# An eight-layer attention and feed-forward model on one core: the second attention's last batch by single tiles, with the next layer's short chain between its units, and four edits elsewhere

## The chip, the cores and the metric

The kernel runs as one program on one core of one Trainium2 chip. The metric is the device time of an execution in microseconds (us), and shorter is better. A measurement of this kernel can tell a difference of about 0.2% from none.

A core has five engines that work side by side, each through its own queue of instructions, in order: TensorE (PE, matrix products, with its weight loads shown apart as PEld), VectorE (DVE), ScalarE (ACT), GpSimd (POOL) and SyncE (SP), which here only starts transfers (DMAs). Matrix products land in PSUM, eight banks of 128 x 512 floats; everything else on chip lies in SBUF.

## The reference

Four batches of 256 tokens with 256 features (x) and of 512 context rows with 128 features (ctx) go through eight layers, all in float32. Each adds to x what it computes of the normalized x:

```python
x = x + L0_xattn(layernorm(x), ctx)    # a0: 16 heads of 16, q and k normalized per head
x = x + L0_ffn(layernorm(x))           # f0: 1024 hidden, the 2 largest of every 4 kept
x = x + L1_xattn(layernorm(x), ctx)    # a1: 16 heads of 128, rms norm of q and k per head
x = x + L1_ffn(layernorm(x))           # f1: below
x = x + L2_xattn(layernorm(x), ctx)    # a2: 16 heads of 128, keys and values shared by two
x = x + L2_ffn(layernorm(x))           # f2: 64 experts, 6 per token, and a shared one
x = x + L3_xattn(layernorm(x), ctx)    # a3: as a2
x = x + L3_ffn(layernorm(x))           # f3: 32 experts, 8 per token
```

The layer f1, which most of the change is about, takes the last token of each batch through a short recurrent chain, the thought, and gives it back to all tokens of its batch:

```python
x_norm = layer_norm(x, in_gamma, in_beta)
thought = x_norm[:, -1, :] @ agg_w + agg_b
for _ in range(4):
    t = layer_norm(thought, pn_gamma, pn_beta)
    t = gelu(t @ d1_w + d1_b)                    # 256 -> 1024
    thought = thought + (t @ d2_w + d2_b)        # 1024 -> 256
broadcast = (thought @ bc_w + bc_b)[:, None, :]
gate = sigmoid(x @ gate_w + gate_b)
return layer_norm(x + gate * broadcast, out_gamma, out_beta)
```

## The kernel before

x lies in SBUF as eight tiles of 128 tokens, two to a batch. The layers are methods of a class `Model` and are written one after the other. What is written first has precedence, but the framework that builds the program fixes the order of each engine's queue itself: it puts an instruction in front of an earlier one that it takes to be not yet ready, if the instruction's buffers are free. Generators (`drain(steps, n)` runs n steps of one) mix work of different stages by hand. A buffer is a slot of a pool; a new tile in a slot waits until the old one has been read for the last time. Pools that open later lie where closed ones lay.

- **Reciprocal roots** (`rsqrt`, L174). A scaling on DVE, then a power of -0.5 on POOL. Every norm uses it: that of tokens, of 128x1 numbers, that of a0's heads of 128x16, that of a1's heads of 128x4.
- **a0** (L245). For batch 0, `made(0)` makes keys and queries, with seven head norms, and `maxima(0)` the scores' maxima. Then `weighted(b)`, some twenty steps of exponentials and value products, runs beside `made(b + 1)` and `maxima(b + 1)`. `beside` (L600) says how many steps of one go with how many of the other (L634, L635).
- **a1** (L766). A group is a batch and four heads. Its unit is one head and one tile of tokens: scores (L833), maximum and exponential (L836, L837), and three units later `finish`: the division, four transposes on PE, and, when two heads of both tiles are there, `pair`: value products (L856) and output products (L865). While a group's eight units run, `prepare` makes the next group's keys and queries a step per unit (`head_rms`, L780).
- **f1** (L1098). Its weights are in three slots of 8 KB per partition, which f0 used before. All eight tiles are normalized and transposed; the four last tokens are gathered by four transfers from the normalized tiles (`last`, L1126); then comes the thought. Between its parts the generator `weight_products` (L900) multiplies a2's weights with each other (wqk and wvo, 28 steps with ten loads of 512 KB through two slots). After the thought, for each batch, `same` spreads its thought over 128 columns, `bc` multiplies it, and for each tile follow gate, sigmoid and the final norm on DVE (L1181 to L1189).
- **a2 and a3** (`gqa`, L950). Each batch begins with a norm and transposes (`begin`, L967), and then come units as in a1, with the queries of two heads at a time (L993). `step` (L1048) runs a step of one of two lists of generators after each unit. a3's `begin` first collects f2's outputs by indirect transfers of POOL (`collect`, L1250), and `fill` is what is left of a3's weight products.
- **f2's weights** (`f2_weights`, L1297) are asked for at a2's beginning, three groups of four experts ahead. **f3's** first weights (`Router.weights`, L1505) have three loads of 1 MB, written after a3's first batch (L1527).

## Time and profile before

| what | us |
|---|---|
| median of three runs | 2515.64 (2515.38 to 2515.76) |
| the profiled execution | 2529.95 |
| its span, first to last instruction | 2528.1 |
| PE busy in it | 2351.8 (93%) |
| DVE, ACT, POOL busy | 1315.4, 909.4, 412.9 |
| DMA mean over the span | 53 GB/s |

The stages' places in the span, by their first and last products on PE: a0's scores from 57.6, f0 from 436.7, a1's scores from 559.6, f1 between a1's last output products (1042.7) and a2's first queries (1165.1), f2's blocks of experts from about 1630, a3's first queries at 1859.7, f3's hidden products from about 2277.

A line of the profile that names a group reads: source line, engine, operation, output and input tiles (with buffer numbers left out), shapes, count, then busy time with the mean of one, then idle time of that engine just before them and what ended it. A line of waits reads: who waited, for whom, us in total, times, the longest. The granted clock is the share of full speed that PE was given. Many of the lines are those of helpers: L172 is every matrix product, L212 every transpose, L165 and L167 the copies out of PSUM, L158 most loads, L180 the power.

### The profile page before, as it was taken

To read this page: it belongs to the slowest core of one execution; us is meant where nothing else is said; L and a number is where in the kernel's file an instruction comes from. 1 tells how busy PE (TensorE), PEld (TensorE's weight loads), DVE (VectorE), ACT (ScalarE), POOL (GpSimd) and SP (SyncE) were. 2 spreads that over 40 slices of the span, in tenths; PEclk is the share of its full clock that TensorE was granted. 3 is DMA by queue.
4 is the path that set the end of the run, shared out by engine and by line. 5 is a ranking of instruction groups with operands and counts; after the bars stand their busy time and mean duration, and the time that the engine had idled before them with its cause. 6 is when DMAs were issued, how large, how long until landed. Compare 5 with 4: busy or idle time off the path is not lost. (4 is left out here: it accounts for less than half of the span.)

```text
span 2528.1 us, 28069 instructions
## 1 busy us (share of the span) xinstructions
PE 2351.8 (93%) x9918; PEld 1474.4 (58%) x9918; DVE 1315.4 (52%) x3490; ACT 909.4 (36%) x1912; POOL 412.9 (16%) x429
## 2 busy tenths in 40 slices
PE   4999998989999999896999999898889999999999
PEld 3555555555555555564656565587756566655555
DVE  5554453877777677526565665311245666641111
ACT  2324323235555555213434343133344344432111
POOL 7303300012212222001020101200120210002222
PEclk7999999999999999888999999999989999999999
DMA  7500001110000000213000000299720000005121
GB/s 233 173 1 1 1 1 37 64 46 1 1 1 1 1 1 1 54 42 104 2 26 1 26 1 25 74 251 267 241 87 2 26 16 11 1 10 162 50 62 35
DMA packets 102424, 134.94 MB, mean 53 GB/s; under 512 B 8272, under 2 KB 82760, under 8 KB 101768
## 3 DMA queue, kind: packets, MB, share of 16 engines
q1 hardware_dynamic: 97672, 120.51, 16.2%
q0 software_dynamic: 4608, 12.59, 1.6%
q8 instruction: 81, 1.33, 0.2%
q14 instruction: 63, 0.52, 0.1%
HBM read 96.50 MB, written 36.57 MB: 53 GB/s over the span
## 5 line engine op out<-in xcount | busy, mean ns | idle before, releaser
L172 PE MATMUL pv_a<-PT_a,ctx 128*128 128x512 f32 x768 | 352.4, 602 | 13.4 <-ACT PT_a L165 4.2
L1011 DVE CUSTOM_DVE_ANT_0 pr_a<-sc_a,mask_a 128x512 f32<-128x512 f32 x256 | 176.0, 688 | 229.3 <-PE sc_a L172 213.4
L172 PE MATMUL sc_a<-ctxT,qT_a 128*128 128x512 f32 x512 | 261.8, 596 | 5.1 <-issue 2.7
L172 PEld LDWEIGHTS pv_a<-PT_a,ctx 128*128 128x128 f32 x768 | 140.4, 191 | 183.7 <-issue 144.7
L1014 ACT ACTIVATE pr_a<-pr_a,sm_a 128x512 f32<-128x512 f32 x256 | 185.0, 723 | 122.6 <-DVE sm_a L1011 96.1
L1019 DVE TENSOR_SCALAR pr_a<-pr_a,sm_a,valid_a 128x512 f32<-128x512 f32 x256 | 140.1, 549 | 6.0 <-DVE sm_a L1018 0.2
L180 POOL TENSOR_TENSOR rstd_f<-rs_f,half 128x1 f32<-128x1 f32 (+1 forms) x36 | 19.2, 548 | 756.5 <-DVE rs_f L179 548.4
L172 PE MATMUL st<-a0qz,a0kT 128*128 128x256 f32 x512 | 132.4, 401 | 9.2 <-ACT pT L582 7.4
L1444 DVE TENSOR_TENSOR h<-u,gs 128x512 f32<-128x512 f32 x48 | 33.2, 691 | 202.3 <-POOL gs L1442 202.3
L172 PE MATMUL sc_a<-kT,qT 128*128 128x512 f32 x256 | 131.4, 595 | 1.3 <-ACT qT L801 0.8
L172 PE MATMUL sc_a<-a0kT,a0qz 128*128 128x496 f32 x256 | 121.1, 597 | 0.0
L172 PEld LDWEIGHTS st<-a0qz,a0kT 128*128 128x128 f32 x512 | 94.9, 197 | 42.6 <-ACT pT L582 22.5
L837 ACT ACTIVATE pr_a<-sc_a,sm_a 128x512 f32<-128x512 f32 x128 | 88.1, 688 | 85.4 <-DVE sm_a L836 84.1
L524 DVE TENSOR_REDUCE a0pad<-sc_a 128x1 f32<-128x496 f32 x128 | 85.8, 672 | 60.4 <-PE sc_a L172 60.0
L180 POOL TENSOR_TENSOR rr_a1k<-rs_a1k,half 128x4 f32<-128x4 f32 x64 | 64.6, 1009 | 320.0 <-DVE rs_a1k L179 290.1
L212 PEld LDWEIGHTS tp_a1p<-ident,pr_a 128*128 128x128 f32 x512 | 63.7, 141 | 67.2 <-issue 42.1
L212 PEld LDWEIGHTS tp_a3p<-ident,pr_a 128*128 128x128 f32 x512 | 64.0, 141 | 65.1 <-issue 50.7
L1441 ACT ACTIVATE gs<-g 128x512 f32<-128x512 f32 x48 | 28.7, 597 | 202.8 <-PE g L172 202.7
L167 DVE COPY xTb_f<-tp_xb_f 128x256 f32<-128x256 f32 x79 | 33.5, 424 | 129.8 <-PE tp_xb_f L212 129.8
L1000 ACT COPY qT_a<-q_a 128x512 f32<-128x512 f32 x64 | 37.5, 585 | 176.4 <-PE q_a L172 158.0
L212 PEld LDWEIGHTS tp_a2p<-ident,pr_a 128*128 128x128 f32 x512 | 63.9, 141 | 61.8 <-issue 48.8
L836 DVE TENSOR_REDUCE sm_a<-sc_a 128x1 f32<-128x512 f32 x128 | 87.4, 683 | 23.0 <-PE sc_a L172 22.9
(481 smaller groups left out, 4648.9 us busy)
## 6 DMA issues: line engine op xcount, KB each, us to landing
sent<-zero SPq DMA_DIRECT2D x6, 2048.0 KB
f2w<-in_L_w1T_dram SPq DMA_DIRECT2D x16, 704.0 KB
f2w<-in_L_w2T_dram SPq DMA_DIRECT2D x16, 704.0 KB
xb_f<-sent SPq DMA_DIRECT2D x20, 512.0 KB
back<-yb_f SPq DMA_DIRECT2D x20, 512.0 KB
cb_f<-f3comb SPq DMA_DIRECT2D x32, 192.0 KB
cb_f<-f3comb SPq DMA_DIRECT2D x32, 128.0 KB
f3wg<-in_L_wgT_dram SPq DMA_DIRECT2D x3, 1024.0 KB
```

What stands on the lines that cost most here:

```text
L167: self.nc.vector.tensor_copy(out, in_)
L172: self.nc.tensor.matmul(out, lhsT, rhs, start=n == 0, stop=n == last)
L180: self.last_pow = self.nc.gpsimd.tensor_tensor(out, t[:p, :n], self.half[:p, :n], ALU.pow).ins
L212: self.nc.tensor.transpose(ps[:, n * w : (n + 1) * w], block, self.ident[:w, :w])
L524: nc.vector.tensor_reduce(pad[:, h, HD : HD + 1], ps[:, :MAIN], AX.X, ALU.max, negate=True)
L836: nc.vector.tensor_reduce(st[:, 0:1], ps, AX.X, ALU.max, negate=True)
L837: nc.scalar.activation(pr, ps, AF.Exp, bias=st[:, 0:1], accum_out=st[:, 1:2])
L1000: nc.scalar.copy(qT, ps.rearrange("p (m t) -> p m t", m=2))
L1011: self.last_unit = nc.vector.tensor_tensor_reduce(pr, ps, mask, -1.0, -3 * NEG, ALU.add, ALU.min, accum_out=st[:, 0:1]).ins
L1014: nc.scalar.activation(pr, pr, AF.Exp, bias=st[:, 0:1], scale=-1.0, accum_out=st[:, 1:2])
L1019: nc.vector.tensor_scalar(pr, pr, st[:, 0:1], valid, ALU.mult, ALU.mult)
L1444: nc.vector.tensor_tensor(h, pu, t, ALU.mult)
```

## The change

Five edits are joined.

1. In a0's `made(0)`, `rsqrt` computes Sqrt on ACT and a reciprocal on DVE in place of the scaling and the power. A dictionary `roots` holds the two small constants and is emptied after `made(0)`.
2. `beside` in a0 runs one step of `weighted` with each step of `made` and with each five of `maxima`, instead of two with three and two with five.
3. The last batch of a1 runs in two passes over all sixteen heads, the second tile of tokens (the last tokens) first. `prepare` makes each group's keys in the first pass, keeps them for the second (two more buffers, `kept`) and makes the queries of one tile; two of its steps go with each unit. `four` replaces `pair` there: it works when four heads of one tile are there. When the last tokens' tile has its sum, f1's thought starts: `thinking` is a generator of 17 steps, and one runs after each unit that follows. f1's weights are asked for at a1's beginning (`load_f1`).
4. f1 normalizes the tiles, then mixes what is left of the thought with a2's weight products, three steps to one, computes the gates of all tiles, and only then `bc`. `out_beta` is added to x on POOL ahead, and the final norm is written as two fused DVE operations. The gate's multiplication is on POOL for the last three batches. Only batch 0's last steps are done in f1; the other six tiles' (`unfinished`) go between a2's first units, and f2's first three weight groups after them. Gates and normalized tiles lie where these groups will lie (`slots`).
5. f3's first loads are ordered behind the last load of a weight product (`last_product`), and in `gqa` the rest of a3's weight products (`fill`) is written ahead of the first batch's `begin`.

```diff
     def load(self, t, src):
-        self.nc.sync.dma_start(t, src)
+    def load(self, t, src, behind=None):
+        inst = self.nc.sync.dma_start(t, src).ins
+        if behind is not None:
+            self.tc.add_manual_dep(inst, behind, ORDER, reason="the other is wanted first")
+        self.last_load = inst.name
         return t
...
         p = var.shape[0]
+        if self.roots:
+            root = self.stats.tile([P, H], F32, tag="root", name=f"root_{name}")
+            self.nc.scalar.activation(root[:p, :n], var, AF.Sqrt, bias=self.roots[eps][:p], scale=scale)
+            self.nc.vector.reciprocal(out, root[:p, :n])
+            return
         t = self.stats.tile([P, H], F32, tag="rs", name=f"rs_{name}")
...
             drain(made(0))
+            self.roots = {}
...
-                    beside(steps, 2, made(b + 1), 3)
-                    beside(steps, 2, maxima(b + 1, "lane1"), 5)
+                    beside(steps, 1, made(b + 1), 1)
+                    beside(steps, 1, maxima(b + 1, "lane1"), 5)
...
+            def four(b, h, i, wT):
+                po = self.held(f"pv_a1_{b}_{h}_{i}")
+                self.matmuls(po, [(self.ctx[:, b, kt, :], wT[:, kt].rearrange("p h t -> p (h t)")) for kt in range(NKT)])
+                outT = p.tile([P, 2, S], F32, tag="outT", name=f"outT_a1_{b}_{h}_{i}").rearrange("p m (a t) -> p (m a) t", a=2)
+                self.copy(outT, po.rearrange("p (h t) -> p h t", h=4))
+                yield
+                if h == 3:
+                    self.total = self.longest(f"o_a1_{b}_{i}")
+                for m in range(4):
+                    nc.tensor.matmul(
+                        self.total[:, :D], outT[:, m, :], wvo[:, h - 3 + m, :],
+                        start=h == 3 and m == 0, stop=h == H - 1 and m == 3,
+                    )
+                if h == H - 1:
+                    self.add_to_x(b * NI + i, self.total[:, :D])
+                    if i == NI - 1:
+                        self.thoughts = self.thinking()
...
-            groups = [(b, hg) for b in range(B) for hg in range(H // HG)]
+            last_passes = ((NI - 1,), *((i,) for i in range(NI - 1)))
+            groups = [
+                (b, hg, which)
+                for b in range(B)
+                for which in ((tuple(range(NI)),) if b < B - 1 else last_passes)
+                for hg in range(H // HG)
+            ]
...
-                        drain(steps, 1)
+                        drain(steps, 1 if len(which) == NI else 2)
+                        if self.thoughts is not None:
+                            drain(self.thoughts, 1)
...
-            drain(begin(0))
             if fill is not None:
                 drain(fill)
+            drain(begin(0))
...
+    def thinking(self):
+        nc, p = self.nc, self.thought_pool
+        STEPS, NH, EPS = 4, 1024 // P, 1e-6
+        w, d1, d2, rows, d1b = self.f1_weights
+        last = p.tile([B, D], F32, name="last")
+        for b in range(B):
+            nc.sync.dma_start(last[b : b + 1, :], self.x[(b + 1) * (S // P) - 1][P - 1 : P, :])
...
+        yield
+        t = p.tile([B, D], F32, tag="t", name="t_in")
+        self.normalize(last, last, 1e-5, "f1last")
+        layer_norm(t, last, rows["in_gamma"], rows["in_beta"], "f1in")
+        yield
+        tT = columns(t, "f1in")
+        yield
+        thought = p.tile([B, D], F32, name="thought")
+        ps = self.work("agg")
+        self.matmuls(ps[:B, :D], [(tT[:, k, :], w[:, 0, k, :]) for k in range(NK)])
+        nc.vector.tensor_tensor(thought, ps[:B, :D], rows["agg_b"], ALU.add)
+        for step in range(STEPS):
+            t = p.tile([B, D], F32, tag="t", name=f"t_{step}")
+            layer_norm(t, thought, rows["pn_gamma"], rows["pn_beta"], f"f1_{step}")
+            yield
+            tT = columns(t, f"f1_{step}")
+            yield
+            ps = self.work(f"d1_{step}")
...
+            nc.scalar.activation(act, hid, AF.Gelu)
+            yield
+            ps = self.work(f"d2_{step}")
+            self.matmuls(ps[:B, :D], [(act[:, n, :], d2[:, n, :]) for n in range(NH)])
+            nc.vector.tensor_tensor(thought, thought, ps[:B, :D], ALU.add)
+            nc.vector.tensor_tensor(thought, thought, rows["d2_b"], ALU.add)
+        yield
+        self.thought_columns = columns(thought, "f1th")
...
+            while next(thoughts, "end") != "end":
+                drain(products, 3)
+            drain(products)
+            for i in range(NT):
+                ps = self.work(f"gate_{i}")
+                self.matmuls(ps[:, :D], [(self.tokens(xnT, k, i * P, P), w[:, 2, k, :]) for k in range(NK)])
+                nc.vector.tensor_tensor(gates[i], ps[:, :D], rows["gate_b"], ALU.add)
+                nc.scalar.activation(gates[i], gates[i], AF.Sigmoid)
+                nc.gpsimd.tensor_tensor(self.x[i], self.x[i], rows["out_beta"], ALU.add)
...
+            def last_steps(tiles):
+                for i in tiles:
+                    o = gates[i]
+                    nc.vector.tensor_tensor(o, o, xn[i], ALU.add)
...
+                    nc.vector.bn_stats(bn, o)
+                    nc.vector.bn_aggr(mv, bn)
+                    self.rsqrt(r, mv[:, 1:2], 1.0, EPS, f"f1o_{i}")
+                    nc.vector.scalar_tensor_tensor(o, o, mv[:, 0:1], out_gamma, ALU.subtract, ALU.mult)
+                    nc.vector.scalar_tensor_tensor(self.x[i], o, r, self.x[i], ALU.mult, ALU.add)
+                    yield
...
+                for i in range(b * NI, (b + 1) * NI):
+                    (nc.gpsimd if b else nc.vector).tensor_tensor(gates[i], gates[i], spread, ALU.mult)
+                if b == 0:
+                    drain(last_steps(range(NI)))
+            self.unfinished = last_steps(range(NI, NT))
...
+        load = lambda t, src: model.load(t, src, model.last_product if g == 0 else None)
```

## The prediction

> **What bounds the kernel now.** I read the page's slices first (is there an engine that is always busy, and where is it not), then busy time by stage, then what ended the waits in the stages where TensorE (PE) is not busy, then the DMA issues there.
>
> ```profile
> span 2528.1 us, 28069 instructions
> ...
> PE   4999998989999999896999999898889999999999
> ```
>
> PE is the bound nearly everywhere. A change gains only in the stretches below nine tenths: the first slice, slices 17 to 19 (the second feed-forward, f1) and some near slice 29. Busy time by stage, the columns being stretch, length, then PE, weight load, DVE, ACT, POOL, granted clock, DMA share, GB/s:
>
> ```profile
> 1042.70:1165.10 122.40, 86.24 (x412) 58.38 (x412) 58.57 (x195) 20.01 (x40) 11.03 (x21) 0.76 0.20 53
> ...
> 1062.00:1133.00 71.00, 65.56 (x332) 44.15 (x333) 20.66 (x56) 14.27 (x27) 2.12 (x4) 0.82 0.20 54
> 1133.00:1165.10 32.10, 10.90 (x42) 7.70 (x40) 27.87 (x107) 3.08 (x7) 6.26 (x12) 0.69 0.06 15
> 551.00:1042.70 491.70, 483.51 (x1912) 278.65 (x1911) 342.94 (x782) 253.53 (x526) 100.59 (x104) 1.00 0.00 1
> 57.50:434.00 376.50, 353.52 (x1683) 213.49 (x1682) 175.53 (x325) 131.43 (x243) 77.86 (x59) 0.98 0.11 35
> 0.00:57.50 57.50, 24.10 (x82) 17.78 (x83) 28.80 (x94) 14.59 (x28) 44.29 (x64) 0.75 0.73 222
> 1815.40:1859.70 44.30, 26.74 (x131) 18.40 (x129) 7.77 (x20) 15.48 (x28) 21.43 (x23) 0.81 0.73 238
> ```
>
> The second attention (551 to 1042.7) leaves PE 8 us. f1 (1042.7, the last output products of that attention, to 1165.1, the third attention's first queries) takes 122.4 us with PE busy 86.2 at a clock of 0.76: the middle is dense, the last 32 us belong to DVE. The start and the opening of the fourth attention (1815.4 to 1859.7) are half empty. What PE waits for in f1, and DVE in the start:
>
> ```profile
> PE tp_a L981 <- DVE xn_a L205: 11.1, 2, 10.1
> PE bc L172 <- DVE rs_f1o L179: 9.5, 1, 9.5
> PE tp_a2wk L212 <- DMA a2wk<-in_L_xattn_Wk_dram: 3.7, 1, 3.7
> ```
>
> ```profile
> DVE a0pad L380 <- POOL var_a0k L180: 9.4, 4, 3.1
> DVE a0pad L380 <- POOL var_a0q L180: 5.1, 2, 2.6
> DVE t_kd L372 <- PE ps_kd L172: 3.5, 1, 3.5
> DVE a0pad L380 <- POOL var_kd L180: 2.7, 1, 2.7
> ```
>
> In f1 it is DVE's eight last steps; in the start it is POOL's seven powers of 2.9 us. The SyncE queue in the fourth attention's opening has two of f3's three loads of 1 MB between the loads that PE waits for:
>
> ```profile
> 1819.86 0.46 SPq L158 DMA_DIRECT2D f3wg<-in_L_wgT_dram  x1
> 1823.32 0.37 SPq L158 DMA_DIRECT2D a3wq<-in_L_xattn_Wq_dram  x1
> 1826.54 0.35 SPq L158 DMA_DIRECT2D a3wv<-in_L_xattn_Wv_dram  x1
> 1826.94 0.43 SPq L158 DMA_DIRECT2D f3wu<-in_L_wuT_dram  x1
> 1839.46 4.36 SPq L158 DMA_DIRECT2D a3wo<-in_L_xattn_Wo_dram  x2
> ```
>
> The sum goes against the profiled execution, 2529.95 us (span 2528.1); the median of the three runs, 2515.64, is 14.3 lower, and I carry the difference over to it unchanged.
>
> **1. Start: Sqrt on ACT and a reciprocal on DVE for POOL's power.** Gone: seven powers of 128x16 (mean 2.90, 20.3 us of POOL) and seven scalings of 0.16 on DVE. Added: seven ACT operations like the 128x32 activation of f1 (0.23) and seven reciprocals like 128x16 at L509 (0.25); two memsets (0.1 each, nothing waits). DVE waited 17.2 us for the powers; a handover now costs about 0.6 (0.23, 0.25 and the starts), 4.2 in all: 13 us gained. ps_kd waited 3.5 for a POOL copy queued behind a power: 2 more. I take -15. At most both waits go, -20.7; at least half remains as waits for PE at its 0.75 clock or ACT's turn, -8. Sqrt needs a table load that the start does not have (1.283 us each); one falls before the first exponential, which at 56.27 is not what the first scores wait for.
>
> **2. First attention, one step of weighting for each other step instead of two for three (and for five).** The same work; about four more of the 20 steps of a batch lie under the making of keys and queries. In 57.5 to 434 PE is idle 23 us, of it 9.2 on th_a0k for a0pad and 7.4 on st for pT. If all of that went, -16; if the 32 maxima of 0.67 us, which get those steps no longer, wait instead, +7. I take -3, nearer to nothing, since 7.4 of it waits for ACT and stays.
>
> **3. Last batch of the second attention by tiles.** Scores, transposes, value products (four 512-wide per four units either way) and output products are the same in number. The first pass has all 16 key tiles and 4 query tiles beside 16 units instead of 32. By intervals of the timeline a unit holds PE 2.7 us (0.86 scores, 0.53 transposes, 0.86 values, 0.43 output), a key tile 1.4, a query tile 2.25: 74 us; DVE's share is 16 x 1.75 + 20 x 1.52 = 58, so PE stays the bound. Cost 0; up to +8 if the banks run short, -3 if the tail shrinks.
>
> **4. The thoughts inside it.** The generator begins at the fifth unit of the second pass, so 12 of its 17 steps run there: agg (1.9), three d1 (3.85 each), two d2 (3.6), four transposes (0.3) are 22 us on a PE with 8 us to spare: **+22**. Their DVE work (four norms of 2.3, adds) and three Gelus lie beside: ACT is busy 253 of 492. Each Gelu takes 0.23 and two loads of 1.283; exponentials behind it come 2.8 late, while a unit's result is used three units later. Stalls +3 (0 to +15; the upper end is four norm chains of 4.3, the time from L1167 at 1099.05 to tp_f at 1103.35, less their overlap). The row after a load shows no more than the load: 1171.32 plus 1.28, next activation 1172.62. The Trainium skill (ScalarE: Activation LUTs, What ACT_TABLE_LOAD costs) puts a switch at about 2.66 us, with a drain of 1.38, and its rule, to batch by table set, speaks against a Gelu between exponentials. By that figure the six switches would hold ACT 16 us instead of 7.7; the sum is the same as long as PE does not wait.
>
> **5. f1.** PE work left at full clock: 16 transposes 2.1, 32 gate products 6.8, weight products 22.3 (48 transposes at 1.04 for eight, 64 at 2.05 for sixteen, 16 at 1.98 for four), the last five thought steps 12, bc 3.4: 46.6 us. At a clock of 0.85 (0.82 now in the dense part) 55. Add the old 2 us of output products, 2 for the first load, and the end: bc to queries. That is spread 0.4, two tiles' multiply, add, statistics 2.3, aggregate and scale 0.3, power 0.7, two fused steps 0.8, then statistics to xn 1.7, transposes and copy 1.3, with 1 for POOL: 8.6. Together 68 us against 122.4: **-54**, at best -66 (clock 0.95, end under the products), at least -38. Two covers: the first load of a2wk goes out behind four loads of 0.43 instead of eleven and the four rows of `last` (issue 1052.57), so its 3.7 us mostly go; if not, +3.7 is in the bound. And POOL gets eight adds and six multiplies of 128x256 (0.72 each, row L457): behind them queue the two powers of the third attention's first norm, at worst 4.3 us late, 1 taken. The Trainium skill (SBUF — State Buffer, Summary: rules for kernel authors) says that DVE with two SBUF inputs and a GpSimd operation that reads SBUF block each other, the later fully. By that, 10 us of POOL work could hold DVE as long; no row here shows such a block.
>
> **6. Third attention.** Six last steps (two adds or statistics of 0.41, 0.3 of small ones, two fused of 0.48: 2.1 us) fall into the first seven units: 12.6 us of DVE, where DVE is busy 26.7 of 50 and 27 us hold 12.4 free. +3 (0 to 12.6). f2's first weight groups are asked for some 30 us later; they are wanted at 1630.
>
> **7. Fourth attention's opening.** f3's 3 MB go behind the last a3wo, the products ahead of the first norm. f3 begins about 2277, so its loads have 400 us of cover; without it, 10 us at 300 GB/s. PE needs 22.3 for the products from 1815.5; with 1 us between groups and first waits of 3, the queries could begin at 1848.7 instead of 1859.7. The gathers (12 of 1.3 on POOL from 1820.4, then norm, transposes, copy) allow 1842.1 at best. -11 (-17.6 to +3, if the norm's transposes now wait behind wvo).
>
> **Sum:** -15 - 3 + 22 + 3 - 54 + 3 - 11 = -55: 2475 profiled, **2460** as median.
>
> **Rivals.** (a) Load-bound products: each 512 KB took 3.7 (a2wo, 1115 to 1119) to 6.8 us (a2wq, 1053.2 to 1060) from issue to use, two at a time; ten at 6.8 are 34 us where PE needs 22: +12, 2472. For it: PE waited for a2wo; against: gates and thoughts can fill. (b) Start and fourth opening don't move, because the load of the weights and the gathers end last there: +26, 2486. Against: POOL's powers are what DVE waited for. (c) More: start -20, f1 at its best: 2443. (d) Slower: in the last batch the four work banks run short, since a norm holds one from matmul to multiply (0.86, 0.69, 0.68, 0.15, 1.0, 0.69 and handovers, 4.5 us) and 1.25 of them come per unit, beside a score bank for 2.5: 8.1 bank-us per unit, 2.0 over four banks, against 4.6 of PE. It decides once each of the 32 units loses 1.75 us; at 2.5 each, 80 us, the median is 2541. (e) The reordering is undone by the queues' fixed order, no change: 2516.
>
> **How the numbers follow.** Likeliest 0.42 (2460, alone 2449 to 2470), a 0.20, b 0.14, c 0.15, d 0.06, e 0.03. The range goes from below c to above b, 2432 to 2490; only d, e and tails lie outside. Faster by over 0.2%, which is what runs of this kernel can tell from none: 0.91; same 0.03; slower 0.06.
>
> **What would show it.** First scores near 42 instead of 57.6; the second attention 20 to 30 us longer with Gelus before its end; f1, from output products to queries, 60 to 75 us with no gap like 9.5 at bc; f3wg issued after the last a3wo and first queries there about 33 us after the first a3wk transposes. Wrong it is if the second attention grows by over 45, if the powers' waits return as waits for ACT, or if f1 shows DMA waits at every product.

## The result and the profile after

| | before, us | after, us | ratio, 95% interval |
|---|---|---|---|
| first set of runs (medians of 4 each) | 2515.51 (2514.96 to 2515.76) | 2471.55 (2465.20 to 2476.43) | 0.9826 (0.9803 to 0.9849) |
| third set of experiments, another chip (medians of 9 and 5) | 2537.19 (2525.57 to 2540.55) | 2490.99 (2477.24 to 2493.99) | 0.9823 (0.9799 to 0.9847) |

The change makes the kernel 44 to 46 us faster. The forecast was 55 (2460); its range held the time. As the stages show, the nearness is in part luck: errors of opposite signs met in the sum.

The page of the changed kernel, its first lines:

```profile
span 2463.4 us, 28085 instructions
...
PE   7999998989999999988999999898899999999999
```

PE's first slice has gone from four tenths to seven and f1's deepest slice from six to eight. Busy time by stage, the columns being stretch, length, PE, weight load, DVE, ACT, POOL, granted clock, DMA share, GB/s:

```profile
1047.90:1122.70 74.80, 54.65 (x256) 40.43 (x255) 32.59 (x98) 17.92 (x34) 16.25 (x25) 0.79 0.48 130
522.70:1047.90 525.20, 510.39 (x2045) 293.79 (x2046) 348.90 (x810) 257.05 (x529) 99.96 (x106) 0.99 0.00 1
39.60:397.80 358.20, 345.97 (x1683) 211.44 (x1682) 174.12 (x325) 133.78 (x246) 76.26 (x58) 0.99 0.12 43
0.00:39.60 39.60, 21.35 (x83) 16.18 (x84) 30.25 (x95) 16.10 (x36) 23.79 (x55) 0.87 0.83 262
1756.60:1796.00 39.40, 26.74 (x129) 18.54 (x128) 9.91 (x26) 15.48 (x28) 21.60 (x22) 0.83 0.68 211
```

These are f1, the second attention, the first attention, the start, and the fourth attention's opening. f1 still leaves PE 20.2 us idle, the opening 12.7. Cut at the first and last products of each stage on PE (and, for the opening, at the second half of the a3wk transposes), the two profiles compare so:

| stage | forecast of the difference | before | after | difference |
|---|---|---|---|---|
| start, to the first scores | -15 | 57.6 | 39.6 | -18.0 |
| first attention, to its last output products | -3 | 376.9 | 358.2 | -18.7 |
| f0 and the second attention's opening | 0 | 125.1 | 124.9 | -0.2 |
| second attention, first scores to last output products | +25 | 485.1 | 525.2 | +40.1 |
| f1, to the third attention's first queries | -54 | 120.4 | 74.9 | -45.6 |
| third attention, to its last output products | +3 | 429.3 | 412.7 | -16.6 |
| f2, to the second half of a3wk | 0 | 221.1 | 221.2 | +0.1 |
| fourth attention's opening, to its first queries | -11 | 44.2 | 39.4 | -4.8 |
| fourth attention and f3 | 0 | 668.5 | 667.4 | -1.1 |

They add up to the 64.7 us between the two spans, which is some 20 more than the medians say. The third attention's 16.6 was not expected and has to be explained first.

What DVE waits for in the start now:

```profile
DVE bn_a L216 <- DMA x<-in_x_dram: 2.1, 1, 2.1
DVE a0bvs L646 <- PE columns L371: 1.4, 1, 1.4
DVE t_kd L390 <- PE ps_kd L182: 1.1, 1, 1.1
DVE var_a0k L395 <- ACT sq_a0k L392: 1.0, 2, 0.5
```

POOL's powers are gone from that list, and the wait for ACT that takes their place is 1.0 us. What PE waits for in f1 now:

```profile
PE tp_a L1046 <- DVE mv_a L217: 6.1, 1, 6.1
PE tp_a2wk L227 <- DMA a2wk<-in_L_xattn_Wk_dram: 4.0, 1, 4.0
PE a2wvo L182 <- DMA a2wo<-in_L_xattn_Wo_dram: 3.5, 3, 1.9
PE tp_f L227 <- DVE mv_f L217: 2.5, 2, 2.3
```

The 9.5 at bc is gone, and of the 11.1 at the third attention's norm 7.2 are left (6.1 here, and 1.1 further down the list); the rest are loads and f1's own norms. SyncE's queue in the fourth attention's opening:

```profile
1765.31 0.37 SPq L165 DMA_DIRECT2D a3wq<-in_L_xattn_Wq_dram  x1
...
1772.15 0.38 SPq L165 DMA_DIRECT2D a3wo<-in_L_xattn_Wo_dram  x1
...
1778.86 10.30 SPq L165 DMA_DIRECT2D a3wo<-in_L_xattn_Wo_dram  x3
1789.21 0.50 SPq L165 DMA_DIRECT2D f3wg<-in_L_wgT_dram  x1
```

f3's loads are behind the last a3wo, as forecast.

### The profile page after: what moved, and what is told of

Same layout as the page of the kernel before. It is cut to its first block, busy times and chain, and to the rows that moved or that the text cites. A ratio compares the mean times of both kernels' runs of the same rounds, so it can differ in the third digit from the quotient of the medians.

```text
span 2463.4 us, 28085 instructions
## 1 busy us (share of the span) xinstructions
PE 2340.3 (95%) x9918; PEld 1472.9 (60%) x9918; DVE 1309.6 (53%) x3474; ACT 919.7 (37%) x1926; POOL 404.0 (16%) x435
## 5 line engine op out<-in xcount | busy, mean ns | idle before, releaser
L182 PE MATMUL st<-a0qz,a0kT 128*128 128x256 f32 x512 | 126.6, 392 | 6.7 <-ACT pT L600 4.3
L195 POOL TENSOR_TENSOR rr_a1k<-rs_a1k,half 128x4 f32<-128x4 f32 x64 | 64.7, 1012 | 309.4 <-DVE rs_a1k L194 284.0
```

The lines of the kernel that those rows point to most:

```text
L182: self.nc.tensor.matmul(out, lhsT, rhs, start=n == 0, stop=n == last)
L195: self.last_pow = self.nc.gpsimd.tensor_tensor(out, t[:p, :n], self.half[:p, :n], ALU.pow).ins
```

## The experiments

My theory after seeing both traces: the gain is the start and the first attention (36.7), and the last batch with its thoughts gives back most of what f1 wins. Rivals: the third attention really is faster; the first attention is shorter only because of the start before it; the second attention's growth is the thoughts alone.

The stages of every profile, in us (the kernels are told below; "opening" is the fourth attention's; the fourth attention itself was 410.2 to 411.4 and f3 257.0 or 257.1 in all of them):

| kernel | start | 1st att. | f0 | 2nd att. | f1 | 3rd att. | f2 | opening |
|---|---|---|---|---|---|---|---|---|
| e_before_again | 57.6 | 375.6 | 125.0 | 485.1 | 121.1 | 411.3 | 222.2 | 44.2 |
| e_beside_alone | 57.9 | 359.1 | 125.0 | 484.5 | 120.5 | 411.8 | 227.5 | 46.2 |
| e_no_roots | 58.0 | 360.8 | 126.3 | 525.2 | 71.5 | 412.5 | 225.9 | 41.5 |
| e_without_a1f1 | 40.5 | 359.9 | 126.4 | 484.5 | 120.7 | 411.2 | 221.6 | 39.5 |
| e_thoughts_late | 39.6 | 359.5 | 126.2 | 498.5 | 130.6 | 411.4 | 226.3 | 40.6 |
| e_gates_first | 39.5 | 359.7 | 126.2 | 525.1 | 67.1 | 410.9 | 222.5 | 40.3 |
| e_beta_later | 37.9 | 353.6 | 124.9 | 526.8 | 70.6 | 412.7 | 227.2 | 40.3 |
| e_both_f1 | 38.8 | 360.0 | 126.2 | 528.4 | 66.1 | 411.1 | 228.2 | 42.6 |
| e_f3_loads_free | 42.5 | 356.5 | 124.9 | 526.8 | 70.3 | 431.6 | 229.4 | 44.4 |
| e_begin_first | 42.4 | 356.7 | 124.9 | 525.1 | 74.9 | 429.9 | 223.4 | 41.4 |
| e_after_again | 39.7 | 358.1 | 124.9 | 525.1 | 71.5 | 431.1 | 217.9 | 39.3 |
| e_best | 41.6 | 358.9 | 126.4 | 525.7 | 66.7 | 427.1 | 227.8 | 40.8 |

The first four ran on one chip, the next four on a second, the last four on a third.

**e_before_again: the kernel before, profiled again.** No edit.

> The kernel before, profiled once more. In the profile of before, three stretches of the third attention (1300 to 1350, 1400 to 1450, 1500 to 1550), where POOL sends f2's rows, have PE idle for 4.0 to 5.0 us each, 13.9 us in the stage; the profiled execution stands 14.3 us above the median. Theory: these stalls belong to that one execution and not to the kernel. Then this profile, if it is near the median of 2515.5, has the third attention (first queries to last output products) at about 415 instead of 428.9. Rival: they belong to the kernel before, and the change took them away. Then they are here again, the stage is 428.9, and the profiled execution is again some 14 us above the median or the median holds them too. The time itself: 2515 to 2516 by both.

Measured: 2515.47 (2507.03 to 2523.22, ten runs) against 2519.18 (2511.05 to 2528.48) for the same kernel beside it, ratio 0.9989 (0.9965 to 1.0013). Two of the three stretches in which POOL sends f2's rows, first in the profile that the prediction was made from, then here (columns as above):

```profile
1300.00:1350.00 50.00, 45.98 (x181) 28.32 (x180) 27.47 (x106) 17.91 (x40) 11.96 (x12) 0.97 0.09 32
1400.00:1450.00 50.00, 45.01 (x180) 27.59 (x179) 29.51 (x119) 17.81 (x42) 11.78 (x12) 0.97 0.09 32
```

and the same two in this experiment:

```profile
1300.00:1350.00 50.00, 50.00 (x202) 30.85 (x201) 32.15 (x119) 21.20 (x47) 11.96 (x12) 1.00 0.09 32
1400.00:1450.00 50.00, 49.98 (x203) 30.93 (x202) 31.56 (x119) 21.20 (x47) 11.77 (x12) 1.00 0.09 32
```

The same kernel does the same work with the stalls and without. In the last set all four profiles, of four different kernels, have the third attention at 427 to 432; in the two sets before it all eight have it at 411 to 413. The times of the kernel before go the same way: 2519 and 2513 in the first two sets, 2537 in the last. So it goes by the set, that is by the chip or the hour, and not by the kernel: the third attention is the same in both, and the profile that I predicted from had 17 to 18 us in it that the changed kernel's profile had not. The record does not say on which chip that profile was taken. Without the stage's 16.6 the spans differ by 48, near what the medians say. What differs there stays open. The experiment also says how well a time can be told: ten runs of the kernel against fifteen of itself have an interval of 0.48%, more than the 0.2% that the prediction started from; and f2's stage, which was to stay as it is, went from 217.9 to 229.4 between the profiles.

**e_beside_alone: the kernel before with edit 2 alone.**

```diff
-                    beside(steps, 2, made(b + 1), 3)
-                    beside(steps, 2, maxima(b + 1, "lane1"), 5)
+                    beside(steps, 1, made(b + 1), 1)
+                    beside(steps, 1, maxima(b + 1, "lane1"), 5)
```

> The kernel before with only the two numbers of beside changed (one step of weighting with each step of making, instead of two with three; one with each five maxima instead of two). My prediction gave this edit -3: 2513. The traces say that the first attention's body (first scores to last output products) fell from 376.5 to 357.8. Theory: the edit alone does that, by 18.7: 2497, with the waits of th_a0k for a0pad down from 9.2 to about 2 and those of st for pT from 7.4 to about 4. Rival: the body is shorter since the start before it is (the clock and the first loads), then it stays above 370 here and the time is 2510 to 2515.

Measured: 2499.51, ratio 0.9911 (0.9883 to 0.9939); the first attention takes 359.1 instead of 375.6 on the same chip, with the start at 57.9. The rival is out. The first attention as a stretch in this run:

```profile
57.90:417.00 359.10, 347.26 (x1683) 211.97 (x1682) 173.82 (x324) 132.32 (x243) 76.39 (x59) 0.98 0.11 36
```

and two of its waits:

```profile
PE st L172 <- ACT pT L582: 3.9, 3, 1.6
PE th_a0k L391 <- DVE a0pad L380: 2.0, 1, 2.0
```

In the first profile of before the two waits were 7.4 and 9.2, and PE was busy 353.9 us for the same 1683 products (57.6 to 434.5). So of the 17.8 between the two stages 11.1 are idle time and 6.7 are PE's busy time. Against e_before_again, on the same chip, it is 16.5, of which 11.3 are idle (23.1 to 11.8) and 5.2 busy (352.5 to 347.3). The products themselves did not get shorter: one of st takes 396 ns in both, one of sc 601 and 602. So their records overlap more when there are fewer waits between them; why the busy time falls by just this much is not shown.

**e_no_roots: the changed kernel with POOL's powers back.**

```diff
-            for eps in (EPS, 1e-5):
-                self.roots[eps] = one([P, 1], f"eps{eps}")
-                nc.vector.memset(self.roots[eps], eps)
```

> The changed kernel with POOL's powers back in the making of batch 0. Theory (and my prediction's first step, 15): first scores at 57.6 again instead of 39.6, 15 to 18 us more than the changed kernel, 2487 to 2490. Rival: the start of the span is bound by loads or the clock, and most of the shift comes back in the body of the first attention: under 8 us more, below 2480.

Measured: 2489.25, ratio 0.9877 (0.9835 to 0.9919), 29.9 under the kernel before on that chip, where the whole change was 44 and 46 under it on others: by this edit 1 is worth 14 to 16, but that compares chips, and the interval here is 10 us to either side. The profiles say it more surely: the first scores are at 58.0 here, as in the kernel before (57.6 to 57.9), and at 37.9 to 42.5 wherever the edit is in, at 40.5 on this chip; the stages behind show nothing that comes back. The rival is out.

**e_without_a1f1: the kernel before with edits 1, 2 and 5 alone.** The diff is that of these edits above.

> The kernel before with edits 1, 2 and 5 alone (start, beside, the fourth attention's opening); the second attention's last batch, the thoughts and f1 are as before. By the stages of the two profiles these three edits are worth 18.0, 18.7 and 4.8, the rest of the change 5.5: 2515.5 - 41.5 = 2474, within 10 us of the changed kernel. By my prediction's terms (15, 3 and 11) it is 2486.5, and the large part of the change is worth 26 to 29. If both are wrong because the start's and the body's gains overlap, it is above 2490.

Measured: 2474.28, ratio 0.9822 (0.9778 to 0.9865), against 0.9826 and 0.9823 for the whole change. The stages are those of before in the second attention and f1 (484.5 and 120.7) and those of the changed kernel elsewhere. The large part of the change, last batch by tiles, thoughts inside, new f1, is thus worth nothing that these times can tell: it costs 40 to 41 in the second attention and wins 46 to 50 in f1. By the stages 5 to 9 us are left, less than the interval of 0.9% can show.

**e_thoughts_late: the changed kernel, the thoughts only in f1.**

```diff
-                        if self.thoughts is not None:
-                            drain(self.thoughts, 1)
...
             while next(thoughts, "end") != "end":
-                drain(products, 3)
+                drain(products, 2)
```

> The changed kernel, but the thoughts' generator is run only in f1 (two steps of products to one of the thought), so that the last batch of the second attention runs by tiles without them. In the changed kernel the stage from first scores to last output products grew by 40.5 (484.7 to 525.2), where I had 22 for the thoughts' PE work and 3 for stalls. Theory: the thoughts' PE work is 24.5 by the timeline, and the tiles' order itself costs some 8 to 12 (head norms that wait for DVE): the stage is 493 to 500 here, f1 grows from 74.8 to 110 to 120, and the time is 5 to 20 above the changed kernel, 2476 to 2491. Rival 1: the order costs nothing and the thoughts disturb the units: the stage is 485 to 489. Rival 2: the order costs nearly all: 510 or more.

Measured: 2489.57 (2480.47 to 2501.95), ratio 0.9904 (0.9870 to 0.9939). The second attention takes 498.5; the stage as a stretch:

```profile
525.40:1023.90 498.50, 484.52 (x1896) 276.98 (x1896) 337.66 (x772) 249.72 (x519) 97.22 (x101) 1.00 0.00 1
```

and what PE waited for in the last batch:

```profile
PE t_a1q L824 <- DVE nrm_a1q L818: 3.8, 4, 1.1
PE t_a1k L824 <- DVE nrm_a1k L818: 2.4, 4, 1.0
PE t_a1k L824 <- DVE rs_a1k L194: 2.1, 3, 0.8
```

Before, the stage had the same 1896 products in 485.1, with PE busy 480.2. So the order by tiles costs 13.4 by itself, 9.1 of it idle: PE's queue comes to the transposes of a head norm before DVE is done with it. The keys' waits (4.5 above) lie in the first pass, three of the four for queries in the second. The thoughts inside cost the rest, 525.2 - 498.5 = 26.7. Both rivals are out. f1 became longer than I had thought, 130.6, and longer than the 120.4 of the kernel before. That is not idle time, which is 33.9 against 36.1, but PE's busy time: 96.7 against 84.3 for the same 404 products, at a granted clock of 0.69 against 0.76. What lowered the clock was not tested.

**e_gates_first, e_beta_later, e_both_f1: f1 in another order.** The first puts what is left of the weight products behind the gates:

```diff
             while next(thoughts, "end") != "end":
                 drain(products, 3)
-            drain(products)
             for i in range(NT):
...
                 if b == 0:
                     drain(last_steps(range(NI)))
+            drain(products)
             self.unfinished = last_steps(range(NI, NT))
```

> The changed kernel with the gates, bc and batch 0's last steps written ahead of the rest of the weight products instead of behind them. In the changed kernel the gates' 32 products stand at 1106.4 to 1113.5, behind the last weight product, and the third attention's first queries 9.3 us behind them, with PE waiting 6.1 and 1.1 for the norm. Theory: the gates' sigmoids and the last steps go beside the ten steps of products (24 us of PE in the trace, 1086 to 1106, less bc), so the 16.3 us from the first gate product to the first query become 7 of gates and 3 for the norm: f1 goes from 74.8 to 62 to 68, time 6 to 12 lower, 2460 to 2466. Rival: the loads of a2wo are what ends f1 (PE waited 3.5 us for three of them, two slots): the products end as late as before and the gates ahead only move the wait; gain under 3 us.

Measured: 2462.12, ratio 0.9800 (0.9770 to 0.9830); f1 67.1. The timeline of PE at the end of f1 in the changed kernel:

```profile
1106.41 7.07 PE L182 MATMUL gate<-f1w,xnT_f 128*128 128x256 f32 x32
1119.55 0.66 PE L1046 MATMUL tp_a<-ident,xn_a 128*128 128x128 f32 x2 [6.07 <-DVE mv_a L217]
1121.33 0.69 PE L1046 MATMUL tp_a<-ident,xn_a 128*128 128x128 f32 x2 [1.12 <-DVE xn_a L220]
```

and in this one the gates and two of the waits behind them:

```profile
1082.55 7.17 PE L182 MATMUL gate<-f1w,xnT_f 128*128 128x256 f32 x32
...
1099.76 1.57 PE L182 MATMUL a2wqk<-a2wkT,a2wqT 128*128 128x128 f32 x8 [2.47 <-DVE a2wqT L177]
...
1106.90 1.96 PE L182 MATMUL a2wvo<-a2wo,a2wvT 128*128 128x512 f32 x4 [1.64 <-DMA a2wo<-in_L_xattn_Wo_dram]
```

The 6.1 at the norm went, 2.5 for a copy that DVE now makes late came, and the loads of a2wo (3.8 in three) stayed. f1 is 4.4 to 7.8 shorter than in the changed kernel's profiles (71.5 to 74.9), as the theory had it, but only 3 us of that are idle time (20.0 and 20.2 there, 17.0 here); the rest is PE's busy time for the same 256 products, at a granted clock of 0.87 against 0.83 and 0.79. The interval of the time holds the changed kernel's ratio, 0.9826.

The second orders POOL's eight additions of out_beta behind the powers of f1's norms:

```diff
+            norms = self.last_pow.name
...
-                nc.gpsimd.tensor_tensor(self.x[i], self.x[i], rows["out_beta"], ALU.add)
+                added = nc.gpsimd.tensor_tensor(self.x[i], self.x[i], rows["out_beta"], ALU.add).ins
+                tc.add_manual_dep(added, norms, ORDER, reason="the norms are wanted first")
```

The timeline of POOL in the changed kernel has there:

```profile
1055.28 2.77 POOL L1266 TENSOR_TENSOR x<-x,out_beta 128x256 f32<-128x256 f32 x4 [3.56 <-DMA f1left<-in_L_ffn_out_gamma_dram]
1058.00 0.55 POOL L195 TENSOR_TENSOR rstd_f<-rs_f,half 128x1 f32<-128x1 f32 x1
```

> The changed kernel with POOL's additions of out_beta ordered behind the powers of f1's token norms. In the changed kernel four of them (2.8 us) begin at 1055.28, 3.6 us after the queue's last work, when the load of the row has landed, and the power of the fourth-last tile follows at 1058.00, for which DVE, and then PE (2.3 us) wait. Theory: PE's waits for mv_f and rs_f in f1 (2.5 and 0.8 us) go, but the load of a2wk ends last there anyway at 1056.8, so the gain is 1 to 3 us: 2468 to 2471. Rival: the thought's chain, not the norms, sets the length there: no change within 1 us.

Measured: 2462.74, ratio 0.9801 (0.9773 to 0.9829); f1 70.6. PE's 2.3 for the norm is gone, but the thought's next norm now costs 2.3 instead of 1.0 in the same place. 70.6 against 71.5 to 74.9 settles nothing; in this run the first attention was 3 to 7 shorter than in others of the same code (PE busy 341.4 there, at a granted clock of 1.00, against 344 to 349 at 0.98 or 0.99), so the time settles nothing either.

> The two edits of f1 together: gates, bc and last steps ahead of the rest of the products, and out_beta behind the norms. Theory: the sum of the two, 7 to 15 below the changed kernel, 2457 to 2465. Rival: the two share a wait (the loads of a2's weights), and it is no better than the better one alone.

Measured: 2464.19, ratio 0.9803 (0.9777 to 0.9829); f1 66.1, in the profile 1.0 better than the gates alone. The rival was nearer; that the two edits share a wait, that for the load of a2wk, is argued and not shown.

**e_f3_loads_free, e_begin_first: the fourth attention's opening, each half undone.**

```diff
-        load = lambda t, src: model.load(t, src, model.last_product if g == 0 else None)
+        load = model.load
```

> The changed kernel without the order of f3's first three loads behind the last load of a weight product. The fourth attention's opening (from the second half of the a3wk transposes to the first queries) is 44.2 in the kernel before, 39.4 in the changed one, where I had forecast 33. Theory: these loads of 3 MB delay a3wq and a3wo, and their order is what gained the 4.8: the opening is 43 to 46 here. Rival: the other half, the fill ahead of the first batch's norm, gained it: 38 to 41 here.

```diff
-            if fill is not None:
-                drain(fill)
             drain(begin(0))
+            if fill is not None:
+                drain(fill)
```

> The changed kernel with the fourth attention's first batch written ahead of the rest of the weight products again, as before, while f3's loads stay behind. Theory: in the changed kernel the norm's transposes stand ahead of a3wvo in PE's queue all the same, and PE waits for them 4.0 and 2.7 us, so this half of the edit gained nothing: opening 38 to 41. Rival: it did, and the opening is 43 or more.

Measured: openings of 44.4 and 41.4, single times 2496.54 and 2488.14. With f3's loads free the opening is that of before; with the first batch written first it stays in the span of the other kernels that have edit 5 (39.3 to 42.6). So, by one profile of each, the loads' order made the gain, and the other half nothing that shows.

**e_after_again: the changed kernel once more.** No edit.

> The changed kernel once more, beside the improved one on the same chip. Single times of it went from 2465 to 2476. Theory: 2466 to 2475, and the stages stay as they were: start 39.6, first attention 358 to 360, second attention 525, f1 71 to 75, third attention 411 to 413, with f2's stage (221 to 228 in the profiles so far) as what differs between executions. Rival: some other stage differs by 5 or more.

Measured: 2490.99, ratio 0.9823 (0.9799 to 0.9847). The rival is right: the third attention takes 431.1 here, the same stalls as in the first profile of before. All other stages agree with the first profile of the changed kernel within 3.4. f1, with the same 256 products, went from 74.9 to 71.5 with the granted clock at 0.83 instead of 0.79; its idle time is the same (20.2 and 20.0).

**e_best: the changed kernel with six edits.** To those of e_both_f1 come:

```diff
             products = self.weight_products(st, "a2")
+            drain(products, 1)
...
-                    (nc.gpsimd if b else nc.vector).tensor_tensor(gates[i], gates[i], spread, ALU.mult)
+                    nc.vector.tensor_tensor(gates[i], gates[i], spread, ALU.mult)
...
-                        drain(steps, 1 if len(which) == NI else 2)
+                        drain(steps, 2 if which == last_passes[0] else 1)
```

and three buffers instead of two for each load of a2's weights.

> The changed kernel with six edits of f1 and of the last batch: gates, bc and batch 0's last steps ahead of the rest of the products; out_beta behind the norms; the load of a2wk ahead of the four rows; three slots instead of two for the loads of a2's weights; the gates' multiplications all on DVE instead of POOL for three batches; one step of preparation per unit in the second pass of the second attention's last batch instead of two. Theory: f1 with the first two is 66.1 us; of it go the waits for a2wk (2.5) and a2wo (3.5) for the most part, and PE's 2.5 for a2wqT, which DVE copies late because its two fused steps take 0.94 and 0.88 instead of 0.48 while POOL multiplies; without POOL's multiplications all of them take 0.48 again. f1 58 to 63, second attention 522 to 524 instead of 525, time 12 to 20 under the changed kernel on the same chip, 2450 to 2460. Rival 1: the fused steps take 0.9 as before, so POOL is not the reason. Rival 2: the thought's chain (its last two parts and bc) ends f1 whatever the loads do: f1 stays above 64.

Measured: 2483.56, ratio 0.9782 (0.9755 to 0.9808), 7.4 under the changed kernel on the same chip, whose ratio is 0.9823. It is the lowest ratio of all, but the two intervals overlap. f1 is 66.7, so the four edits added to e_both_f1 won nothing there, and the theory's 58 to 63 is out. Rival 2's sign came (above 64), but not that the chain ends f1 whatever the loads do: PE's idle time in f1 fell from 15.0 to 13.2, while ten more products lie in it (266 against 256) at a lower granted clock (0.87 against 0.90). The waits for a2wo fell to 0.9, and in their place PE waits 4.0 for the thought's norm (the thought's third part now ends 11.5 us after the last output products, in the changed kernel 2.5) and still 2.7 for the copy of a2wqT, which now stands behind DVE's own multiplications. The second attention is 525.7: one step per unit in the second pass won nothing either. Rival 1 is out, as the part on the chip shows.

## Why the prediction was right, and where not

The time (2471.55 against 2460, range 2432 to 2490) and the sign were right, but the gain does not lie where I had put it. Of my 55 us, 26 were to come from the last batch, the thoughts, f1 and the third attention together (25 - 54 + 3), and there the times can tell no gain and the stages show 5 to 9; the start and the first attention, which I had at 18, gave 34 to 37 by the profiles. That the sum came near is in part luck. Term by term:

1. **Start, -15.** Right, and somewhat larger: 18.0 in the first profiles, 17.5 on one chip (14 to 16 in times, which are less sure). First scores at 39.6; I had said near 42.
2. **First attention, -3.** Wrong by 13 to 16; e_beside_alone shows -16.5 on one chip. The step that failed is "nearer to nothing, since 7.4 of it waits for ACT and stays": it fell to 3.9, and the wait for a0pad to 2.0. The bound of -16 was too narrow as well. It counted idle time only, and PE's busy time, 5 to 7 us less, was not in it.
3. **Last batch by tiles, 0 (at most +8).** Wrong: +13.4. "DVE's share is 58, so PE stays the bound" compared totals. The wait is one of distance: two steps of preparation per unit leave the transposes closer behind their products than DVE's chain is long. That explanation is argued from the waits; e_best lengthens the distance in the second pass alone. There the wait of the queries' transposes fell from 1.7 to 0.7, which speaks for the explanation, but other waits of PE grew by as much and the stage did not become shorter. The first pass was not tried, so the cause stays open. It is rival (d)'s place with 0.42 us per unit (13.4 over 32), below its 1.75.
4. **Thoughts inside, +25.** Right in sum: 26.7. Its parts were not: PE's own work is 25.9 instead of 22, and the stalls are 0.8 instead of 3 (PE's idle time in the stage went from 14.0 to 14.8).
5. **f1, -54.** The mechanism was right, the size 5 to 9 too large: 74.9 and 71.5, where the forecast, cut as in the table, was 66. PE's busy time came as forecast in the first profile (54.7 against 55), and so did the idle time at the end (7.9 in the three waits behind the gates, against 8.6). The steps that failed are the waits before it, 2 in the sum and some 12 in the profile (idle time is 20.2 in all): the load of a2wk, whose 3.7 should mostly go, still cost 4.0; three loads of a2wo, which the sum did not have, 3.5; and f1's own norms, which it did not have either, 4.3. A wait that I had named for POOL's queue (an addition ahead of a power) came, though one norm earlier than I had put it: 2.3. And "no row here shows such a block", of DVE beside POOL, was a misreading of the profile before, as the part on the chip shows; its price was 1.5 us.
6. **Third attention, +3.** Where there are no stalls, 411.2 to 411.8 without the six last steps and 410.9 to 412.7 with them: at most 1.5.
7. **Fourth opening, -11.** Too large: 4.8. I had 1 us between groups and first waits of 3. PE still waited 3.0 for a3wq, 4.0 and 2.7 for the norm's transposes, which stood ahead of a3wvo in its queue, and 2.1 for a3wo, at a clock of 0.83. I had feared the norm waiting behind wvo; it was the other way round.

So the terms 1 and 2 gave about 16 to 19 more than forecast, 3 to 5 about 20 to 24 less, and 7 gave 6 less: some 10 in all, and the time is 11.6 above the forecast. "Second attention 20 to 30 us longer" was wrong (40.1), still under the 45 that I had set for falling; f1 at 60 to 75 held; "first queries about 33 us after the a3wk transposes" was wrong (39.4). Of the rivals, (a) comes nearest in time (2472), but not for its reason alone: loads cost f1 7.5 in all, 2 of which were in the sum, where (a) had 12 more.

## What the runs showed of the chip

**DVE and POOL on the same memory.** Behind bc in the changed kernel POOL multiplies six tiles while DVE runs its fused steps. The timeline of DVE in the changed kernel:

```profile
1113.20 0.83 DVE L1280 SCALAR_TENSOR_TENSOR gate<-gate,mv_f1o,f1left 128x256 f32<-128x256 f32 x1
1114.47 0.94 DVE L1281 SCALAR_TENSOR_TENSOR x<-gate,rstd_f1o,x 128x256 f32<-128x256 f32 x1
1115.42 0.85 DVE L1273 TENSOR_TENSOR f1left<-f1left,f1left 128x256 f32<-128x256 f32 x1
1116.26 0.47 DVE L1280 SCALAR_TENSOR_TENSOR gate<-gate,mv_f1o,f1left 128x256 f32<-128x256 f32 x1
```

and that of POOL at the same time:

```profile
1113.02 0.73 POOL L1293 TENSOR_TENSOR f1left<-f1left,spread 128x256 f32<-128x256 f32 x1 [0.27 <-ACT f1left L1265]
...
1114.40 1.60 POOL L1293 TENSOR_TENSOR f1left<-f1left,spread 128x256 f32<-128x256 f32 x2
```

The same forms take 0.47 to 0.48, and 0.39 to 0.41, when POOL is not multiplying (1116.26), so each takes about twice as long beside it. They do not share, though: each of the three ends 0.28 us behind the end of the POOL multiplication beside it (1114.03 behind 1113.75; 1115.41 behind 1115.13, where the first of the two in POOL's last row ends; 1116.27 behind 1115.99), the fused steps and the addition alike. Half speed for as long as POOL multiplies would have made them about 0.74, 0.96 and 0.69, an estimate from the rows, instead of 0.83, 0.94 and 0.85. So DVE's operation waits for POOL's, and the length that shows is the wait and the work. The second POOL multiplication of that row, which began beside a DVE operation, takes 0.92 instead of 0.73. In e_best, where POOL has no multiplications, all of them are short (timeline of DVE):

```profile
1099.24 0.47 DVE L1282 SCALAR_TENSOR_TENSOR gate<-gate,mv_f1o,f1left 128x256 f32<-128x256 f32 x1
1100.16 0.48 DVE L1283 SCALAR_TENSOR_TENSOR x<-gate,rstd_f1o,x 128x256 f32<-128x256 f32 x1
```

The prediction had weighed the rule of the Trainium skill (SBUF — State Buffer, Summary: rules for kernel authors), that DVE with two SBUF inputs and a GpSimd operation that reads SBUF block each other, and had said that no row shows such a block. That was a misreading: the rows here agree with the rule, and the profile of before has such rows too, in the start (timelines of DVE and of POOL):

```profile
43.32 0.77 DVE L380 TENSOR_TENSOR a0pad<-t_a0q,var_a0q 128x256 f32<-128x256 f32 x1 [2.44 <-POOL var_a0q L180]
44.01 0.82 DVE L411 TENSOR_TENSOR a0kbd<-a0kd,a0quarter 128x256 f32<-128x256 f32 x1
...
45.09 0.41 DVE L411 TENSOR_TENSOR a0kbd<-a0kd,a0quarter 128x256 f32<-128x256 f32 x1
```

```profile
43.21 1.35 POOL L464 COPY a0qz<-qT 32x512 f32<-32x512 f32 x2
```

POOL's second copy ends at 44.56 and the operation beside it at 44.83, 0.27 behind it; alone the same operation takes 0.41. The price in f1 was 1.5 us, in the three operations above and in an addition at 1110.54 (0.62 instead of 0.41), not the 10 that the rule's worst case would have made: only four of DVE's operations were held up by a multiplication of POOL's.

**Table loads.** The thoughts' first Gelu between exponentials, in the timeline of ACT of the changed kernel:

```profile
997.72 0.69 ACT L866 ACTIVATE pr_a<-sc_a,sm_a 128x512 f32<-128x512 f32 x1 [1.55 <-DVE rs_a1q L194]
998.31 0.19 ACT L866 ACTIVATION_READ_ACCUMULATOR pr_a<-sc_a,sm_a 128x1 f32 x1
998.52 1.28 ACT L1224 ACT_TABLE_LOAD   x1
...
1002.24 0.69 ACT L825 ACTIVATE qT<-t_a1q,gqk 128x512 f32<-128x512 f32 x1 [0.95 <-PE t_a1q L824]
1002.95 1.28 ACT L866 ACT_TABLE_LOAD   x1
1004.25 0.69 ACT L866 ACTIVATE pr_a<-sc_a,sm_a 128x512 f32<-128x512 f32 x1
```

Each load begins 0.02 us after the operation ahead of it and the exponential 0.02 after the load: 1.28 per switch. The Trainium skill (ScalarE: Activation LUTs, What ACT_TABLE_LOAD costs) adds a drain of about 1.38 to each; these rows leave no room for one, and the measurement decides. PE waited for ACT at a score once in the whole stage, 0.4 us, at its beginning and long before the first Gelu; the profile of before has the same wait.

**Stalls around indirect transfers.** In the first profile of before and on one chip of three in the experiments, PE loses 3 to 5 us in each stretch of 50 in which POOL issues twelve indirect transfers. DVE has gaps there of up to 8.7 us that end on a remote event; in the eight profiles of the other two chips, and in the first of the changed kernel, it has none. The third attention is 16 to 21 us longer with them, more than most edits here are worth. Whether the chip or something else in that set makes them was not tried.

## What to carry to other kernels

Before a profile is costed edit by edit, take it twice: one stage of this one held 18 us that other profiles of the same kernel did not have, and any change would have seemed to win them. When work is put between the units of a full engine, its own time is easy to forecast (25 against 26.7) and the order that makes room for it is not (0 against 13.4): the waits there say to look at how far an instruction stands behind what it waits for in its queue, and not only at the busy totals. And isolate the parts: two changed pairs of numbers in a loop gave 16 to 20 us, and the rearrangement around the second attention gave none that the times can tell.
